# A linear-attention block with a low-rank feed-forward: one root finder chain for two norms, normalizations one at a time, a reordered first double step

## The chip, the cores and the metric

The kernel runs on one NeuronCore of a Trainium2 chip. The core has five engines with an instruction stream each: TensorE (PE, matrix products; PEld are its weight loads), VectorE (DVE), ScalarE (ACT), GpSimd (POOL), and SyncE (SP), which here issues nearly all DMAs. An engine works its stream strictly in order and waits on semaphores for the others. The metric is the time of one execution on the device, in microseconds (us), as the median of several runs.

## The reference

The input x has 4 sequences of 2048 tokens with 512 features, in float32. A layer norm without weights is followed by a linear attention with 16 heads of 32 features, then a second layer norm and a feed-forward of rank 128; both are added to x.

```python
x = L0_attn_x
x = x + attn(_layernorm(x), ...)
x = x + ffn(_layernorm(x), ...)

def attn(x, ln_g, ln_b, W_qkv, b_qkv, W_gate, b_gate, W_proj, b_proj):
    x_norm = (x - mu) * rsqrt(var + EPS) * ln_g + ln_b
    q, k, v = split(x_norm @ W_qkv + b_qkv, 3)
    gate = sigmoid(x @ W_gate + b_gate)
    gate = gate / (mean(gate) + EPS)
    q = relu(q * gate) ** 2 + EPS
    k = relu(k * gate) ** 2 + EPS
    # over the tokens of a sequence, per head:
    #   kv += k v^T;  ks += k;  out = (q kv) / (q ks + EPS)
    return out @ W_proj + b_proj

def ffn(x, U1, V1, b1, U2, V2, b2):
    P = x @ U1                                # 512 -> 128
    H = gelu(P @ V1 + b1)                     # 128 -> 2048
    return (H @ U2) @ V2 + b2                 # 2048 -> 128 -> 512
```

The attention's own norm sits on top of the first layer norm, so each token needs two reciprocal roots for the first norm: one of var + EPS and one of var (1 + EPS) + EPS². The second layer norm needs one.

## The kernel before

**Tiling.** The 8192 tokens are 64 chunks of 128; a sequence is 16 chunks. x stays in a pool of ten tiles of 128 x 512, loaded chunk by chunk. The main loop takes two chunks per turn, c = 4, 6, ..., 62, a *double step*: it computes gates, values, queries and keys of chunks c and c + 1, the attention of chunks e = c - 1 and c, the output projection of chunks e - 1 and e, the second norm of these two, and the feed-forward of a pair further back. Chunks 0 to 3 are done by straight code ahead of the loop.

**Products.** Pairs of chunks are multiplied by a seven-product scheme (`gates_and_values`, `queries_and_keys`, `project_two_out`): sums and differences of features (`combinations`, tile *combos*, four additions on GpSimd, lines 415 to 418) and of weights (`difference`, slots T1 to T4 of *wgv*, *wqk*, *wp*) take the place of an eighth product. In `gates_and_values` the first product is *ps_g* (from the features themselves), the second *ps_gu* (needs *combos*), then a third, and a fourth and fifth that add to the first and third bank after VectorE has read these (*gu*, lines 443 and 447). All of these matmuls appear on line 423, those of `project` on line 379.

**Attention.** Per chunk: `sums_of` scans the keys (VectorE, L591) and multiplies them by the queries (GpSimd, *qsum* L601); `inverse_denominators` turns *qsum* and inverts (*back* L637 to *inv* L652, VectorE); `scores_of` makes four banks *ps_a* which VectorE masks (L625); `weighted` adds the state's part and the scores' part (*ps_n*, *ps_m*, L687 and L698), divides (*oT*, L661) and updates the state (*ps_S* L717, copied L726). `values_of(c)` makes the values of one chunk by four matmuls on PE (each in two passes) and one addition on VectorE (L551); value tiles come from a pool of three.

**Turning.** Queries, keys and normalized chunks have to be transposed. `blocks` turns 32 x 32 blocks on VectorE (L286, a pool of three tiles), and a write to DRAM and reads in another order do the rest: `turned_in_quarters` writes once (L302) and queues four reads (L307), issued by the next `transfers_back`; `turned` writes four times (L325) and queues one read (L330), issued by `features_back`. All of them go through SP's queue, in order.

**Norms.** Means and variances come from VectorE (`moments`). `first_norm_factors` makes the scale, the shift and the factor *unscale* of the first norm for two chunks, from chunk 8 on all on GpSimd: two variances (L349, L350), a start value from the bits of the number (L242), three Newton rounds of four operations (L247 to L250), two operations for *shift_o* (L260, L261), two for *unscale*. `second_norm` does the same for one variance per chunk (L802, L242, L247 to L250, *shift_f*) and returns two functions, one per chunk, which normalize on ScalarE (L267), add the feed-forward's last bias on GpSimd (L812) and turn the result (*x2T*). `normalize_chunk` normalizes a chunk for the first norm (ScalarE, *xl*) and returns a function that turns it.

**Feed-forward.** `feed_forward(b)` returns a list of 21 pieces for a pair of chunks: `down` (*ps_P* L832 from *x2T*, copied to *pT* L843), 18 times `both(f)` (*ps_h* L847, the gelu *h* on ScalarE L849, and two pieces later *ps_Q* L853 from *h*), and `up` twice. `pump(n)` takes the next n pieces; so they are laid between the attention's products.

**What sets the order.** Nothing is scheduled automatically (`manual_schedule`): each engine's stream is in the order in which the Python code calls, and tiles rotate through small pools, where a new tile waits for the last reader of the one it replaces. The part of a double step that the change touches stands, in calls, as follows: `project_two_in_step(e)`, two pieces, `sums_and_products(c)`, `second_norm([e - 1, e])`, `first_norm_factors([c + 4, c + 5])`, two pieces, `scores_in_step(c)`, `denominators_in_step(c)` (which adds a bias to x on GpSimd, L970), four pieces, both normalizations of the second norm, `combine(c + 2)`, the remaining pieces up to `up`, the attention of c, `up`, `sums_and_products(c + 1)`, `normalize_pair(c + 4)`.

Of the kernel before, what the change touches and what calls it, by code (L numbers as in the profile page):

```python
# [52 lines left out]
ALU = mybir.AluOpType  # L53
# [3 lines left out]
EPS = 1e-5  # L57
# [3 lines left out]
def tile_linear_attention_block(  # L61
# [19 lines left out]
    nc = tc.nc  # L81
# [8 lines left out]
    NJ = 4  # L90
    NP = 2
    BT = NP * P
    NC = B * T // P
# [87 lines left out]
    for g in range(NK):  # L181
        halves = w_proj[bass.ts(g, P), :].rearrange("(two p) n -> two p n", two=2)
        for half in range(2):
            at = (half ^ (g % 2)) * (P // 2)
# [44 lines left out]
    def inverse_root(v, tag, name):  # L229
        n = v.shape[-1]  # L230
        sd = work.tile([P, 2 * NJ], F32, tag="sd", bufs=2, name=f"sd_{name}")[:, 0:n]
        nc.scalar.activation(sd, v, AF.Sqrt)
        rs = work.tile([P, 2 * NJ], F32, tag=tag, bufs=5, name=f"{tag}_{name}")[:, 0:n]
        nc.vector.reciprocal(rs, sd)
        return rs
# [17 lines left out]
    def variances(n, name):  # L253
        return work.tile([P, 2 * NJ], F32, tag="newton_v", bufs=2, name=f"v_{name}")[:, 0:n]

    def normalizer(mean, rs, name, engine):

        n = rs.shape[-1]
        shift = work.tile([P, NJ], F32, tag="shift", bufs=6, name=f"shift_{name}")[:, 0:n]
        engine.tensor_mul(shift, mean, rs)  # L260
        engine.tensor_scalar_mul(shift, shift, -1.0)  # L261
        return rs, shift

    def normalized(src, norm, j, name):
        t = temp(name)
        rs, shift = norm
        nc.scalar.activation(  # L267
            t, src, AF.Identity, scale=rs[:, j : j + 1], bias=shift[:, j : j + 1]
        )
        return t  # L270
# [24 lines left out]
    def transfers_back():  # L295
        while back:
            back.pop(0)()
# [18 lines left out]
    def features_back():  # L316
        while features:
            features.pop(0)()
# [19 lines left out]
    def first_norm_factors(chunks, mv):  # L338

        n = len(chunks)
        at = slice(chunks[0] % NJ, chunks[-1] % NJ + 1)
        name = str(chunks[0])
        inverse, engine = inverse_root_by_steps, nc.gpsimd
        if chunks[0] < 2 * NJ:
            inverse, engine = inverse_root, nc.vector
        v = variances(2 * n, name)
        engine.tensor_scalar_add(v[:, 0:n], mv[:, at, 1], EPS)  # L349
        engine.tensor_scalar(v[:, n:], mv[:, at, 1], 1.0 + EPS, EPS * EPS, ALU.mult, ALU.add)  # L350
        rs = inverse(v, "rs_o", name)
        norm = normalizer(mv[:, at, 0], rs[:, n:], f"o{name}", engine)
        back = work.tile([P, NJ], F32, tag="unscale", bufs=2, name=f"unscale_{name}")[:, 0:n]
        engine.tensor_mul(back, rs[:, 0:n], rs[:, n:])
        engine.tensor_mul(back, back, v[:, n:])
        for n, c in enumerate(chunks):
            first_norm[c] = norm, n, back[:, n : n + 1]
# [18 lines left out]
    def project(c, w, name):  # L376
        ps = bank(name)
        for k in range(NK):
            nc.tensor.matmul(
                ps, xlT_of[c][:, k, :], w[k], start=(k == 0), stop=(k == NK - 1)  # L380
            )
        return ps
# [165 lines left out]
    def values_of(c):  # L548
        ps = project(c, rows_of[2], f"ps_v_{c}")
        values[c] = v = new_values(c)  # L550
        nc.vector.tensor_add(v, ps, bqkv_row[:, 2 * D : 3 * D])  # L551

    def new_values(c):
        return work.tile([P, D], F32, tag="v", bufs=3, name=f"v_{c}")
# [239 lines left out]

    x2T_of = {}

    def second_norm(chunks, mv):

        at = slice(chunks[0] % NJ, chunks[-1] % NJ + 1)
        name = str(chunks[0])  # L800
        v = variances(len(chunks), f"f{name}")
        nc.gpsimd.tensor_scalar_add(v, mv[:, at, 1], EPS)  # L802
        rs = inverse_root_by_steps(v, "rs_f", name)
        norm = normalizer(mv[:, at, 0], rs, f"f{name}", nc.gpsimd)

        def normalize(n, c):
            b, j = divmod(c, NP)
            if b not in x2T_of:
                x2T_of[b] = work.tile([P, NP, NQ, NK, DH], F32, tag="x2T", name=f"x2T_{b}")
            xt = x_of[c]  # L810
            x2 = normalized(xt, norm, n, f"x2_{c}")
            nc.gpsimd.tensor_add(xt, xt, b2_row)  # L812
            to = x2T_of[b][:, j]
            if c < NC - 2:
                turned_in_quarters(x2, to, f"x2_{c}")
                return None

            return lambda: nc.scalar.copy(
                to.rearrange("p i k t -> p k i t"),
                features_first(x2, f"ps_x2_{c}").rearrange("p k (i t) -> p k i t", t=DH),  # L820
            )

        return [lambda n=n, c=c: normalize(n, c) for n, c in enumerate(chunks)]
# [60 lines left out]
    def pump(n):  # L884
        for _ in range(min(n, len(rest))):
            rest.pop(0)()
# [47 lines left out]
    mv_first = mv_second = None  # L934
# [3 lines left out]
    combos = {}  # L938
    results = {}
    waiting = []  # L940

    def combine(c):
        combos[c] = combinations(c)
# [11 lines left out]
    def new_keys_in_step(c):  # L955
        kT = new_keys(c)
        keys_of(kT, pairs[c][2])
        keys[c] = kT, None

    def sums_and_products(c):  # L960
        if c not in keys:
            new_keys_in_step(c)
        kT = keys[c][0]
        keys[c] = kT, sums_of(c, kT, pairs[c][1])

    def scores_in_step(e):
        return scores_of(e, pairs[e][1], keys[e][0])

    def denominators_in_step(e):
        nc.gpsimd.tensor_add(x_of[e], x_of[e], bp_row)  # L970
        return inverse_denominators(e, keys[e][1])
# [22 lines left out]
    def normalize_pair(c):  # L994
        if c < NC:
            return [normalize_chunk(n) for n in (c, c + 1)]
        return []
# [26 lines left out]
    mv = new_moments("mv_0")  # L1024
# [9 lines left out]
    turn_xl = normalize_chunk(1)  # L1034
# [4 lines left out]
    turn_xl = [normalize_chunk(c) for c in (2, 3)]  # L1039
# [24 lines left out]
    second = queries_and_keys(0, combos.pop(0), later=moments_meanwhile)  # L1064
# [7 lines left out]
    turn_xl = normalize_pair(NJ)  # L1072
# [11 lines left out]
    def scores_of_first():  # L1084
# [4 lines left out]
    second = queries_and_keys(  # L1089
        2,  # L1090
        combos.pop(2),
        sums_of_first,
        factors,
        scores_of_first,
        lambda: new_keys_in_step(1),
    )
    inv = denominators_in_step(0)
    rest_of_attention(0, held["scores"], inv)
    sums_and_products(1)
    scores = scores_in_step(1)  # L1100
    combine(NJ)
    new_keys_in_step(2)
    inv = denominators_in_step(1)
    values_of(3)
    project_in_step(0)
    for to in (T1, T2, T4, T3):
        difference(wgv, to, nc.gpsimd)
# [2 lines left out]
    scores = scores_in_step(2)  # L1110
# [10 lines left out]
    for c in range(NJ, NC, 2):  # L1121

        e = c - 1
        for n in (c + 4, c + 5):
            if n < NC:
                load_x(n)
        held = {}

        def denominators():
            held["inv"] = denominators_in_step(e)  # L1130

        later = c == NJ
        if later:
            gates_and_values(c, combos[c], lambda: new_keys_in_step(e))
            sums_and_products(e)
            while waiting:
                waiting.pop(0)()
            transfers_back()
            turn_xl = normalize_pair(c + 2)
        else:  # L1140
            gates_and_values(c, combos[c], denominators)
        scores = scores_in_step(e)

        def turn_features():
            for turn in turn_xl:
                turn()

        second = queries_and_keys(c, combos.pop(c), queries=turn_features if later else None)

        rest += feed_forward((c - 4) // NP)  # L1150
        pump(1)
        if later:
            denominators()
        rest_of_attention(e, scores, held["inv"])
        combine_results(e)
        features_back()
        second()
        for n in (c + 4, c + 5):
            first_moments(n)
        pump(4)  # L1160
        project_two_in_step(e)
        transfers_back()
        pump(2)
        sums_and_products(c)
        waiting += second_norm([e - 1, e], mv_second)
        if c + 4 < NC:
            first_norm_factors([c + 4, c + 5], mv_first)
        pump(2)


        scores = scores_in_step(c)
        inv = denominators_in_step(c)
        pump(4)
        while waiting:
            waiting.pop(0)()
        transfers_back()
        if c + 2 < NC:
            combine(c + 2)
        pump(len(rest) - NP)
        rest_of_attention(c, scores, inv)  # L1180
        if c + 2 < NC:
            pump(len(rest))
            sums_and_products(c + 1)
        for turn in normalize_pair(c + 4):
            turn()


    e = NC - 1
    new_keys_in_step(e)
    scores = scores_in_step(e)  # L1190
# [71 lines left out]
```

## Time and profile before

| | us |
|---|---|
| median of 3 runs | 1853.89 |
| lowest and highest of them | 1851.64, 1854.89 |
| the profiled execution | 1857.51 |
| its span, first to last instruction | 1855.7 |
| TensorE busy in it | 1787.7 |
| VectorE busy | 1321.7 |
| GpSimd busy | 907.2 |
| ScalarE busy | 665.9 |
| mean granted TensorE clock, as a share | 0.996 |

All the times inside an execution come from that one profiled execution, counted from its first instruction. A line of a timeline gives the start, the duration, the engine, the source line, the operation, *written <- read* tiles with their shapes and the number of instructions that were merged, and in brackets the idle time of the engine before it with what ended it. A line of the waits gives who waited for whom, the total in us, how many times, and the longest. A line of the stretches gives the stretch, its length, the busy time of PE, PEld, DVE, ACT and POOL with the number of instructions, the granted TensorE clock as a share, the share of the DMA engines' time, and GB/s. Matmuls overlap in the array, so the durations of neighbours add up to more than the distance of their starts; distances of starts are the better measure.

A steady double step, from one *ps_gu* to the next (1008.56 to 1065.31 us), takes 56.75 us, and 28 to 30 of them make up the loop.

### The profile page before, as it was taken

To read this page: it belongs to the slowest core of one execution; us is meant where nothing else is said; L and a number is where in the kernel's file an instruction comes from. 1 tells how busy PE (TensorE), PEld (TensorE's weight loads), DVE (VectorE), ACT (ScalarE), POOL (GpSimd) and SP (SyncE) were. 2 spreads that over 40 slices of the span, in tenths; PEclk is the share of its full clock that TensorE was granted. 3 is DMA by queue.
4 is the path that set the end of the run, shared out by engine and by line. 5 is a ranking of instruction groups with operands and counts; after the bars stand their busy time and mean duration, and the time that the engine had idled before them with its cause. 6 is when DMAs were issued, how large, how long until landed. Compare 5 with 4: busy or idle time off the path is not lost.

```text
span 1855.7 us, 35857 instructions
## 1 busy us (share of the span) xinstructions
PE 1787.7 (96%) x13112; PEld 1128.1 (61%) x13112; DVE 1321.7 (71%) x2579; ACT 665.9 (36%) x1203; POOL 907.2 (49%) x1761
## 2 busy tenths in 40 slices
PE   9899999999999999999999999999999999999998
PEld 4555666655666556665556665566655566655667
DVE  7887767777768677677777686776777776867662
ACT  4333334333433333343334333333423333333333
POOL 3565454454554455544545544555445455445441
PEclk9999999999999999999999999999999999999999
DMA  7132332323322323322233223232222332232220
GB/s 227 62 105 86 101 99 89 91 87 99 108 90 82 99 86 102 98 90 89 87 99 110 89 82 98 86 103 96 88 91 88 96 111 89 83 98 76 80 81 23
DMA packets 286132, 173.81 MB, mean 94 GB/s; under 512 B 134654, under 2 KB 235518, under 8 KB 285828
## 3 DMA queue, kind: packets, MB, share of 16 engines
q1 hardware_dynamic: 284894, 171.51, 29.6%
q8 instruction: 104, 1.70, 0.4%
q14 instruction: 72, 0.59, 0.1%
q10 hardware_dynamic: 1062, 0.01, 0.0%
HBM read 89.68 MB, written 81.79 MB: 92 GB/s over the span
## 4 chain that ended last, share of the span: by engine, by line
PE 61%; POOL 22%; DVE 10%; issue 6%; ACT 1%; DMA 0%; SPq 0%; DVEq 0%; POOLq 0%; ACTq 0%
PE ps_q L423 11%; PE ps_g L423 8%; PE ps_h L847 4%; POOL x L812 4%; PE ps_gu L423 3%; PE ps_p L423 3%; PE ps_t L423 3%; PE ps_k L423 3%; PE ps_pt L423 3%; PE ps_Q L853 3%; PE ps_P L832 3%; PE ps_v L423 3%; PE ps_gt L423 3%; PE ps_u L423 3%; DVE st L226 2%
## 5 line engine op out<-in xcount | busy, mean ns | idle before, releaser
L849 ACT ACTIVATE h<-ps_h,b_col 128x256 f32<-128x256 f32 x512 | 227.6, 468 | 304.7 <-PE ps_h L847 304.4
L853 PE MATMUL ps_Q<-h,u_sb 128*128 128x256 f32 x1024 | 302.5, 387 | 31.8 <-ACT h L849 31.8
L847 PE MATMUL ps_h<-pT,v_sb 128*128 128x256 f32 x1024 | 302.3, 387 | 1.3 <-DVE pT L843 1.3
L853 PEld LDWEIGHTS ps_Q<-h,u_sb 128*128 128x128 f32 x1024 | 187.4, 190 | 82.8 <-ACT h L849 61.0
L601 POOL TENSOR_TENSOR qsum<-qT,sums 128x512 f32<-128x512 f32 x64 | 75.4, 1178 | 314.7 <-DVE sums L591 310.5
L847 PEld LDWEIGHTS ps_h<-pT,v_sb 128*128 128x128 f32 x1024 | 190.8, 191 | 32.6 <-DVE pT L843 2.8
L423 PE MATMUL ps_q<-wqk,xlT 128*128 128x512 f32 x372 | 179.7, 606 | 2.7 <-DVE t L501 2.6
L625 DVE TENSOR_TENSOR a<-ps_a,causal 128x512 f32<-128x512 f32 x256 | 158.3, 680 | 24.1 <-PE ps_a L615 24.1
L423 PE MATMUL ps_g<-wgv,xlT 128*128 128x512 f32 x360 | 170.0, 601 | 0.9 <-DVE gu L447 0.9
L520 POOL TENSOR_TENSOR u<-u,t 128x512 f32<-128x512 f32 x32 | 40.7, 1272 | 204.4 <-DVE t L518 198.0
L591 DVE TENSOR_TENSOR_SCAN sums<-keep,kT 128x516 f32<-128x516 f32 x64 | 80.1, 1251 | 85.0 <-POOL kT L575 85.0
L567 POOL TENSOR_SCALAR k<-k 128x512 f32<-128x512 f32 x64 | 96.2, 1504 | 82.3 <-DVE blocks_k L286 82.3
L402 ACT ACTIVATE gate<-gate 128x512 f32<-128x512 f32 x64 | 40.2, 629 | 236.7 <-DVE gate L398 236.6
L423 PEld LDWEIGHTS ps_g<-wgv,xlT 128*128 128x128 f32 x360 | 65.9, 190 | 94.6 <-issue 71.8
L470 POOL TENSOR_TENSOR v<-gu,g 128x512 f32<-128x512 f32 x30 | 38.1, 1271 | 167.9 <-DVE g L465 167.9
L423 PEld LDWEIGHTS ps_q<-wqk,xlT 128*128 128x128 f32 x372 | 67.2, 191 | 83.5 <-issue 53.3
L491 ACT ACTIVATE t<-t,rg 128x512 f32<-128x512 f32 x32 | 23.1, 722 | 200.0 <-DVE t L489 200.0
L226 DVE BATCH_NORM_STATS2 st<-x 128x6 f32<-128x512 f32 x128 | 86.6, 676 | 8.6 <-DMA x<-in_L_attn_x_dram 6.4
L495 ACT ACTIVATE k<-u,rg 128x512 f32<-128x512 f32 x64 | 45.7, 714 | 119.1 <-DVE u L489 119.1
L615 PEld LDWEIGHTS ps_a<-qT,kT 32*128 32x128 f32 x2048 | 63.3, 186 | 33.4 <-issue 21.2
L970 POOL TENSOR_TENSOR x<-x,bp_row 128x512 f32<-128x512 f32 x64 | 82.2, 1284 | 0.0
L812 POOL TENSOR_TENSOR x<-x,b_row 128x512 f32<-128x512 f32 x64 | 79.9, 1272 | 0.9 <-ACT x L267 0.9
(199 smaller groups left out, 3673.6 us busy)
## 6 DMA issues: line engine op xcount, KB each, us to landing
x<-in_L_attn_x_dram SPq DMA_DIRECT2D x64, 256.0 KB
dr_q<-blocks_q SPq DMA_DIRECT2D x64, 256.0 KB
dr_k<-blocks_k SPq DMA_DIRECT2D x64, 256.0 KB
qT<-dr_q SPq DMA_DIRECT2D x256, 64.0 KB
kq<-dr_k SPq DMA_DIRECT2D x256, 64.0 KB
out_dram<-x SPq DMA_DIRECT2D x64, 256.0 KB
dr_x<-blocks_x SPq DMA_DIRECT2D x62, 256.0 KB
x2T<-dr_x SPq DMA_DIRECT2D x248, 64.0 KB
```

The costliest lines, as they stand in the source:

```text
L226: nc.vector.bn_stats(st, src)
L423: nc.tensor.matmul(ps, stationary[:, k, :], w[:, slot, k, :], start=(k == 0 and not more), stop=(k == NH - 1), skip_group_check=True,)
L567: nc.gpsimd.tensor_scalar_add(k, k, EPS)
L591: nc.vector.tensor_tensor_scan(sums.rearrange(flat), keep.rearrange(flat), kT.rearrange(flat), 0.0, ALU.mult, ALU.add,)
L601: nc.gpsimd.tensor_mul(qs.rearrange("p k (i t) -> p k i t", t=DH), qT.rearrange("p i k t -> p k i t"), sums[:, :, 1 : P + 1].rearrange("p ...
L615: nc.tensor.matmul(ps[r][:, bass.ts(g, P)], kT[rows, g, 1 : P + 1], qT[rows, :, g, :], start=True, stop=True,)
L625: nc.vector.tensor_tensor(a, ps[r].rearrange("p (g t) -> p g t", t=P), causal.unsqueeze(1).to_broadcast([P, NK, P]), ALU.mult,)
L812: nc.gpsimd.tensor_add(xt, xt, b2_row)
L847: nc.tensor.matmul(ps, v1_sb[:, 0, bass.ts(f, P)], held["p"], start=True, stop=True)
L849: nc.scalar.activation(h, ps, AF.Gelu_apprx_tanh, bias=b1_col[:, f : f + 1])
L853: nc.tensor.matmul(held["q"], u2_sb[:, f, :], held["h"].pop(f), start=(f == 0), stop=(f == NF - 1))
L970: nc.gpsimd.tensor_add(x_of[e], x_of[e], bp_row)
```

## The change

Four things are changed.

- *One chain for both norms.* `second_norm` takes the chunks of the first norm as well (`others`) and their moments. It puts all their variances beside its own in one tile (two columns become six), runs one start value and one set of Newton rounds over all, makes *shift_f*, and then calls the new function `both_factors`, the tail that was part of `first_norm_factors`. The call of `first_norm_factors` in the loop is gone. For the last two double steps there are no others.
- *Normalizations one by one.* Where both functions of the second norm were called together between the feed-forward's pieces, one is called, then two pieces follow, then the other.
- *Ahead of the loop*, `values_of(3)` moves from behind `denominators_in_step(1)` to just ahead of `denominators_in_step(0)` and chunk 0's attention.
- *In the first double step* (c = 4), `sums_and_products(3)` moves from ahead of the scores into `queries_and_keys`, behind the first query's product; the waiting normalizations of chunks 0 and 1 and the reads they queue move behind the first addition of `queries_and_keys`; the normalization and the turns of chunks 6 and 7 move from `queries_and_keys` to behind `second()`, followed by their reads.

```diff
     def first_norm_factors(chunks, mv):
...
-        inverse, engine = inverse_root_by_steps, nc.gpsimd
-        if chunks[0] < 2 * NJ:
-            inverse, engine = inverse_root, nc.vector
+        engine = nc.vector
         v = variances(2 * n, name)
         engine.tensor_scalar_add(v[:, 0:n], mv[:, at, 1], EPS)
         engine.tensor_scalar(v[:, n:], mv[:, at, 1], 1.0 + EPS, EPS * EPS, ALU.mult, ALU.add)
-        rs = inverse(v, "rs_o", name)
+        both_factors(chunks, mv, v, inverse_root(v, "rs_o", name), engine)
+
+    def both_factors(chunks, mv, v, rs, engine):
+        n = len(chunks)
+        at = slice(chunks[0] % NJ, chunks[-1] % NJ + 1)
+        name = str(chunks[0])
         norm = normalizer(mv[:, at, 0], rs[:, n:], f"o{name}", engine)
         back = work.tile([P, NJ], F32, tag="unscale", bufs=2, name=f"unscale_{name}")[:, 0:n]
         engine.tensor_mul(back, rs[:, 0:n], rs[:, n:])
...
-    def second_norm(chunks, mv):
+    def second_norm(chunks, mv, others=(), mv_others=None):
...
-        v = variances(len(chunks), f"f{name}")
-        nc.gpsimd.tensor_scalar_add(v, mv[:, at, 1], EPS)
+        n, m = len(chunks), len(others)
+        v = variances(n + 2 * m, f"f{name}")
+        nc.gpsimd.tensor_scalar_add(v[:, 0:n], mv[:, at, 1], EPS)
+        if others:
+            var = mv_others[:, others[0] % NJ : others[-1] % NJ + 1, 1]
+            nc.gpsimd.tensor_scalar_add(v[:, n : n + m], var, EPS)
+            nc.gpsimd.tensor_scalar(
+                v[:, n + m :], var, 1.0 + EPS, EPS * EPS, ALU.mult, ALU.add
+            )
         rs = inverse_root_by_steps(v, "rs_f", name)
-        norm = normalizer(mv[:, at, 0], rs, f"f{name}", nc.gpsimd)
+        norm = normalizer(mv[:, at, 0], rs[:, 0:n], f"f{name}", nc.gpsimd)
+        if others:
+            both_factors(others, mv_others, v[:, n:], rs[:, n:], nc.gpsimd)
...
         lambda: new_keys_in_step(1),
     )
+    values_of(3)
     inv = denominators_in_step(0)
     rest_of_attention(0, held["scores"], inv)
...
     inv = denominators_in_step(1)
-    values_of(3)
     project_in_step(0)
...
         if later:
             gates_and_values(c, combos[c], lambda: new_keys_in_step(e))
-            sums_and_products(e)
-            while waiting:
-                waiting.pop(0)()
-            transfers_back()
-            turn_xl = normalize_pair(c + 2)
+
+            def normalized_first():
+                while waiting:
+                    waiting.pop(0)()
+                transfers_back()
+
+            scores = scores_in_step(e)
+            second = queries_and_keys(
+                c,
+                combos.pop(c),
+                first=normalized_first,
+                queries=lambda: sums_and_products(e),
+            )
         else:
             gates_and_values(c, combos[c], denominators)
-        scores = scores_in_step(e)
...
-        second = queries_and_keys(c, combos.pop(c), queries=turn_features if later else None)
+            scores = scores_in_step(e)
+            second = queries_and_keys(c, combos.pop(c))
...
         second()
+        if later:
+            for turn in normalize_pair(c + 2):
+                turn()
+            features_back()
...
-        waiting += second_norm([e - 1, e], mv_second)
-        if c + 4 < NC:
-            first_norm_factors([c + 4, c + 5], mv_first)
+        others = [c + 4, c + 5] if c + 4 < NC else []
+        waiting += second_norm([e - 1, e], mv_second, others, mv_first)
         pump(2)
...
         pump(4)
-        while waiting:
-            waiting.pop(0)()
+        waiting.pop(0)()
+        pump(2)
+        waiting.pop(0)()
         transfers_back()
```

More of the change, by code (lines that the diff above doesn't have):

```diff
@@ L1134, in tile_linear_attention_block @@
             gates_and_values(c, combos[c], lambda: new_keys_in_step(e))
-            sums_and_products(e)
-            while waiting:
-                waiting.pop(0)()
-            transfers_back()
-            turn_xl = normalize_pair(c + 2)
+            def normalized_first():
[9 more added lines that the diff above has]
+            )
         else:
             gates_and_values(c, combos[c], denominators)
-        scores = scores_in_step(e)
-        def turn_features():
-            for turn in turn_xl:
-                turn()
-        second = queries_and_keys(c, combos.pop(c), queries=turn_features if later else None)
+            scores = scores_in_step(e)
+            second = queries_and_keys(c, combos.pop(c))
         rest += feed_forward((c - 4) // NP)
```

## The prediction

> **What bounds the kernel now.** First the page's busy shares and its chain that ended last; the chain names the engines that set the end.
>
> ```profile
> PE 1787.7 (96%) x13112; PEld 1128.1 (61%) x13112; DVE 1321.7 (71%) x2579; ACT 665.9 (36%) x1203; POOL 907.2 (49%) x1761
> PE 61%; POOL 22%; DVE 10%; issue 6%; ACT 1%; DMA 0%; SPq 0%; DVEq 0%; POOLq 0%; ACTq 0%
> ```
>
> TensorE (PE) is busy for 96%, so without new arithmetic there are at most 1855.7 - 1787.7 = 68 us to win. But 22% of the chain is GpSimd (POOL), which is busy for only 49%: it matters somewhere. The view of waits, PE alone, says where PE stands still; its first two rows hold 47.7 us:
>
> ```profile
> PE ps_Q L853 <- ACT h L849: 31.8, 30, 1.1
> PE ps_gu L423 <- POOL combos L416: 15.9, 28, 1.1
> ```
>
> Both come once per double step. The timelines of PE, POOL and ACT in one ordinary double step (56.75 us long) show them:
>
> ```profile
> 1054.92 0.23 POOL L349 TENSOR_SCALAR v<-mv 128x2 f32<-128x2 f32 x1
> 1055.21 0.19 POOL L350 TENSOR_SCALAR v<-mv 128x2 f32<-128x2 f32 x1
> 1055.48 0.19 POOL L242 TENSOR_SCALAR rs_o<-v 128x4 int32<-128x4 int32 x1
> ...
> 1054.87 1.52 ACT L267 ACTIVATE x<-x,shift_f,rs_f 128x512 f32<-128x512 f32 x2 [1.14 <-POOL shift_f L261]
> 1056.30 1.18 ACT L849 ACTIVATE h<-ps_h,b_col 128x256 f32<-128x256 f32 x3
> ...
> 1056.81 0.70 PE L853 MATMUL ps_Q<-h,u_sb 128*128 128x256 f32 x2 [1.05 <-ACT h L849]
> 1057.34 0.59 PE L847 MATMUL ps_h<-pT,v_sb 128*128 128x256 f32 x2
> ...
> 1006.17 1.88 PE L423 MATMUL ps_g<-wgv,xlT 128*128 128x512 f32 x4
> 1008.56 1.98 PE L423 MATMUL ps_gu<-wgv,combos 128*128 128x512 f32 x4 [0.51 <-POOL combos L416]
> 1010.38 1.88 PE L423 MATMUL ps_g<-wgv,combos 128*128 128x512 f32 x4
> ```
>
> GpSimd's root finder for the second norm ends with shift_f; ScalarE waits for it, normalizes two chunks, and only then makes the h that PE's ps_Q needs. GpSimd meanwhile does a second root finder (rs_o), three additions and the combinations, and PE's ps_gu waits for these. Last, PE in the first double step, whose order also changes, with the stretch view of the granted clock:
>
> ```profile
> 75.38 5.40 PE L379 MATMUL ps_v<-wgv,xlT_early 128*128 128x512 f32 x8 [3.66 <-DVE oT L661]
> 100.62 1.98 PE L423 MATMUL ps_g<-wgv,xlT 128*128 128x512 f32 x4 [0.61 <-DVE gu L447]
> 113.38 3.53 PE L423 MATMUL ps_q<-wqk,xlT 128*128 128x512 f32 x4 [2.60 <-DVE t L501]
> ...
> 75.56:78.97 3.41, 3.41 (x5) 1.35 (x6) 3.41 (x7) 0.00 (x0) 1.84 (x2) 0.50 0.25 75
> 113.11:116.52 3.41, 3.14 (x4) 1.51 (x5) 0.90 (x2) 0.00 (x0) 0.70 (x1) 0.50 0.24 73
> ```
>
> After both long stalls the granted clock (the column before the last two) is 0.50 for 3.41 us: four matmuls take 3.53 us instead of 1.88, so such a stall costs up to 1.7 us more.
>
> **One chain for both norms** (28 double steps, c = 4 to 58). Removed from GpSimd: one start value (L242) and 12 steps. From L349 at 1054.92 to the end of unscale at 1060.03 the old stretch takes 5.1 us, from v_f at 1050.42 on 9.61 us. The new one: three variances 0.86, L242 0.28, 12 steps on 6 columns, four operations for shift_f and shift_o and two for unscale, together 1.48. A step takes 0.2775 us on 2 columns and 0.2817 on 4 (3.33 and 3.38 us for 12), so I take 0.286 on 6, 3.43 us. Sum 6.05, so all behind it comes 3.56 us earlier. L416 ended at about 1008.51; it will end at 1004.95, and PE wants ps_gu at 1006.17 + 1.82 = 1007.99. The wait is gone with 3.0 us to spare. Price: a stall is worth its idle time, 0.06 of modelled end (2.39 us from ps_g to ps_gu, instead of 1.82 and 0.51) and 0.10 of refill (ps_gu to the next 1.82, otherwise 1.72). So 15.9 + 28 x 0.16 = **-20.4 us**. What is hidden now: VectorE's sums wait for kT L575 behind these combinations (3 us each); they come earlier too, and PE's next look at VectorE (gu L447) gets easier.
>
> **The two normalizations, one by one.** shift_f now stands behind two more variances and wider steps: 0.56 + 0.10 + 0.01 = 0.67 us later. ScalarE's first normalization starts at 1055.54 instead of 1054.87; the next h no longer waits for the second (0.715): 1056.255 against 1056.30, and ps_Q starts 0.05 us earlier. The second normalization now stands between the h: it begins at 1056.965, the h behind it at 1057.68, its ps_Q at 1058.19, where PE wants 1058.165: 0.03 lost. Net -0.02 x 28 = **-0.6 us**. Bounds: were the second normalization to hide fully and shift_f late by nothing, -0.7 each, which the POOL rows exclude; I take -0.25 to +0.35 each, -7 to +10. The later second turn (VectorE blocks_x +1.35 us, then its copy on SP and eight x2T reads) lies 20 us ahead of its reader ps_P, and GpSimd reaches the addition that must follow it (L812) at 1058.97, after 1057.7. For c = 60 nothing is fused: 0.7 us gained, **-0.7**; for c = 62 the tail's ps_P waits 2.01 us for the x2T transfer, which does not move: 0.
>
> **First double step.** (a) values_of(3) moves ahead of chunk 0's attention. Its 8 matmuls (3.43 us) fill the idle time before 75.38. But v_3 takes the buffer of v_0 (a pool of three), so VectorE's addition L551 waits until chunk 0's last ps_S matmul: 68.47 (the end of ps_q at 66.75 + 1.72) + 3.43 + 1.4 (ps_n to ps_S) = 73.3, with its own 0.65 us 74.0. Behind it in VectorE's order stand back L637 (71.76 before, now 74.0), inv, oT, sums; behind sums GpSimd's qsum, combinations, the wgv differences (10.39 us) and qsum of chunk 2; behind that gu L447 and PE's ps_g at 100.62. All slip by 2.25: PE waits until 102.87, idle 3.2 us. (b) Putting sums and the turns behind the score products frees t L501: the stall of 2.60 at 113.38 and its half clock go. From 102.87 the unstalled sequence (11.72 us) brings ps_t to 114.6, or 116.3 after a half clock, against 116.74. (c) The same move makes the turns of x2 late: behind t L501, 3.6 to 5.3 us later. The eight x2T reads moved 75 GB/s from 113 to 120 and now land at 123.6 to 125.3, so ps_P, at 123.61 before, starts at 123.8 to 125.5, a half clock (1.7) possible behind it. (d) The turns of chunks 6 and 7, with eight writes and two reads on SP, now follow second(): 1.43 us on ScalarE ahead of h (at most 0.4 seen by PE), and blocks_xl of chunk 7 uses the buffer of blocks_q of chunk 5, whose write queues behind the kq reads: 1 to 2 us on VectorE, which then holds PE's output products. Sum of (c) and (d) at the ends: 0.2 + 0 and 1.9 + 1.7 + 2.4; the low end is below nothing if the late turns hide, -2. I take **+2.6**, range -2 to +6.
>
> The Trainium skill (page "TensorE: Matmul & The Clock Gate", section "HAM oscillation — how this bites in real kernels") says that only idle gaps above about 3.4 us throttle PE again. Here a stall of 2.60 us did, so the trace decides. By that rule the stalls of (a) and (c) would cost no half clock, and the sum would be about 1 us lower.
>
> **Sum:** -20.4 - 0.6 - 0.7 + 2.6 = -19.1 us against the profiled execution: span 1855.7 to 1836.6, its 1857.5 us to 1838.4. That execution lay 3.6 us above the median of the runs; on their scale 1853.9 - 19.1 = **1834.8**.
>
> **Rivals.** *The h wait goes as well.* If the root chain's extra 0.67 us is hidden, ps_Q gains 0.7 per step: 1834.8 - 20 = 1815. For it: 31.8 us stand in that row. Against it: the 1.14 us that ScalarE idles for shift_f is time measured from shift_f, and that is later. 7%.
> *The gain is given back at the second normalization.* If ScalarE has no slack there, each step loses up to 0.715 - 0.13 = 0.58: +16, 1851. For it: ScalarE feeds PE one h per 0.86 us in this place. Against: three h follow each other at 0.355. 5%.
> *Half clock in every step (slower).* A stretch of 3.41 us with 1.51 us idle (58.50 to 61.91) kept the full clock, one with 2.33 lost it. If the wait at ps_Q grows from 1.07 past about 1.75, that is by 0.67 and no h moved ahead, each step pays 1.7 more: 28 x (1.7 + 0.67) = 66, so 1835 + 66 = 1901. It decides from 0.7 us more idle; I find 0.05 less. 5%.
> *It doesn't do what it says.* If combos L415 waits for something other than its own engine, say the xlT transfer, the 20.4 stay: 1855. Against: its row of waits names only ACT, once. 3%.
>
> **How the numbers follow.** Forecast 80%, 1834.8; its own bounds are 1834.8 - 4.6 - 6.4 and + 3.4 + 10.6 if the two uncertain terms both end at one side, which is unlikely, so 1827 to 1843 in most cases. The range, 1825 to 1843, takes in these and the way towards the first rival; the other rivals (13%) and the far corners stay out. 0.2%, 3.7 us, is what a measurement can tell from no change: faster holds the forecast, the first rival and a little of the second, 88%; same the rest of the second and part of the fourth, 6%; slower 6%.
>
> **What would show it.** Right: no PE row for combos L416; POOL some 364 instructions fewer; PE's idle time at ps_Q near 1.0 per step; a double step of 56.1 us; PE waiting near 102 for gu L447 and near 123 for x2T. Wrong: a new row of PE with 28 entries, 0.50 of the clock inside the loop, or a double step still at 56.75.

## The result and the profile after

The changed kernel takes 1828.99 us (median of 4 runs, 1826.79 to 1830.76) where the kernel before takes 1854.37 on the same chip: a ratio of 0.9866, 95% interval 0.9848 to 0.9883. The 25.4 us are more than the 19.1 that were forecast, and the time lies 5.8 us under the forecast 1834.8. A second set of runs of the changed kernel gave 1828.23 and 0.9861 (0.9845 to 0.9878).

The page of the changed kernel (busy shares, the chain that ended last), and its view of waits, PE alone:

```profile
span 1825.0 us, 35492 instructions
PE 1776.5 (97%) x13112; PEld 1133.1 (62%) x13112; DVE 1320.5 (72%) x2579; ACT 659.8 (36%) x1203; POOL 834.6 (46%) x1397
PE 91%; DVE 4%; ACT 1%; issue 1%; DMA 1%; POOL 1%; SPq 0%; ACTq 0%; DVEq 0%; POOLq 0%
```

```profile
PE ps_Q L865 <- ACT h L861: 25.4, 30, 1.1
PE ps_g L426 <- DVE gu L450: 3.6, 1, 3.6
PE ps_P L844 <- DMA dr_q<-blocks_q: 2.5, 1, 2.5
PE ps_P L844 <- DMA out_dram<-x: 2.4, 1, 2.4
PE ps_p L740 <- DVE oT L664: 2.3, 1, 2.3
```

GpSimd issues 364 instructions fewer (1761 to 1397) and has left the chain that sets the end (22% to 1%). The row *ps_gu <- combos* with its 28 entries is gone; the row *ps_Q <- h* is still there, a fifth smaller. Of the four rows below it, *gu*, *dr_q* and *oT* belong to the first double step and the stretch ahead of it, *out_dram* to the tail. The wait put down to *dr_q* is that of *ps_P* for *x2T*: SP issues the eight reads of *x2T* from 116.68 us on, and *dr_q* right behind them, at 121.30; in the profile with values_of(3) late, below, the same wait is put down to *x2T*. So of the signs named ahead, the missing row, the 364 instructions and the waits near 102 and 123 came; the idle time at *ps_Q* came out at 0.87 instead of 1.0 per step and the double step at 55.72 instead of 56.1, as the next lines show.

One ordinary double step of the changed kernel, from its timelines of PE, ACT and POOL:

```profile
1050.04 1.88 PE L426 MATMUL ps_gu<-wgv,combos 128*128 128x512 f32 x4
1096.35 0.59 PE L859 MATMUL ps_h<-pT,v_sb 128*128 128x256 f32 x2
1097.81 0.70 PE L865 MATMUL ps_Q<-h,u_sb 128*128 128x256 f32 x2 [0.87 <-ACT h L861]
1098.78 1.59 PE L865 MATMUL ps_Q<-h,u_sb 128*128 128x256 f32 x6
1100.30 0.31 PE L690 MATMUL ps_n<-qT,S 32*32 32x128 f32 x4
1105.76 1.88 PE L426 MATMUL ps_gu<-wgv,combos 128*128 128x512 f32 x4
...
1096.59 0.81 ACT L267 ACTIVATE x<-x,shift_f,rs_f 128x512 f32<-128x512 f32 x1 [1.66 <-DVE inv L655]
1097.31 0.82 ACT L861 ACTIVATE h<-ps_h,b_col 128x256 f32<-128x256 f32 x2
1098.02 0.81 ACT L267 ACTIVATE x<-x,shift_f,rs_f 128x512 f32<-128x512 f32 x1
...
1096.33 0.23 POOL L261 TENSOR_SCALAR shift_f<-shift_f 128x2 f32<-128x2 f32 x1
1101.91 0.73 POOL L419 TENSOR_TENSOR combos<-combos,xlT 128x256 f32<-128x256 f32 x1
```

The double step takes 1105.76 - 1050.04 = 55.72 us, 1.03 less than before. The combination that *ps_gu* reads ends at 1101.91 + 0.73 = 1102.64, 3.1 us ahead of its reader. ScalarE starts the first normalization at 1096.59, as *shift_f* ends at 1096.56 (the view names VectorE's *inv*, which happened to end at 1096.58; with five Newton steps, below, the same row names *shift_f*, long after *inv*). The h then come between the two normalizations, as the order has it.

### The profile page after: what moved, and what is told of

Read it like the earlier page. It is cut to its first block, busy times and chain, and to the rows that moved or that the text cites. A ratio compares the mean times of both kernels' runs of the same rounds, so it can differ in the third digit from the quotient of the medians.

```text
span 1825.0 us, 35492 instructions
## 1 busy us (share of the span) xinstructions
PE 1776.5 (97%) x13112; PEld 1133.1 (62%) x13112; DVE 1320.5 (72%) x2579; ACT 659.8 (36%) x1203; POOL 834.6 (46%) x1397
## 4 chain that ended last, share of the span: by engine, by line
PE 91%; DVE 4%; ACT 1%; issue 1%; DMA 1%; POOL 1%; SPq 0%; ACTq 0%; DVEq 0%; POOLq 0%
PE ps_Q L865 13%; PE ps_h L859 12%; PE ps_q L426 11%; PE ps_g L426 11%; PE ps_a L618 4%; PE ps_u L883 3%; PE ps_pt L426 3%; PE ps_p L426 3%; PE ps_t L426 3%; PE ps_k L426 3%; PE ps_v L426 3%; PE ps_u L426 3%; PE ps_gt L426 3%; PE ps_pv L426 3%; PE ps_P L844 3%; PE ps_gu L426 3%
## 5 line engine op out<-in xcount | busy, mean ns | idle before, releaser
L865 PE MATMUL ps_Q<-h,u_sb 128*128 128x256 f32 x1024 | 304.7, 388 | 25.4 <-ACT h L861 25.4
L426 PE MATMUL ps_g<-wgv,xlT 128*128 128x512 f32 x360 | 166.2, 597 | 3.6 <-DVE gu L450 3.6
```

Of the source, the lines that this page charges most:

```text
L426: nc.tensor.matmul(ps, stationary[:, k, :], w[:, slot, k, :], start=(k == 0 and not more), stop=(k == NH - 1), skip_group_check=True,)
L865: nc.tensor.matmul(held["q"], u2_sb[:, f, :], held["h"].pop(f), start=(f == 0), stop=(f == NF - 1))
```

## The experiments

Each kernel was run beside the kernel before on the same chip. First, what each part is worth in a double step. Distances of starts on PE, in us, in one ordinary step (c = 36, in the changed kernel c = 38):

| stretch of the double step | before | one chain alone | one by one alone | changed | both later |
|---|---|---|---|---|---|
| ps_gu to ps_gt | 7.16 | 6.87 | 7.16 | 6.86 | 6.86 |
| ps_gt to ps_pt | 23.46 | 23.46 | 23.47 | 23.47 | 23.46 |
| ps_pt to ps_u (holds ps_Q) | 21.93 | 22.42 | 21.30 | 21.85 | 20.61 |
| ps_u to the next ps_gu | 4.20 | 3.54 | 4.76 | 3.54 | 3.54 |
| whole step | 56.75 | 56.29 | 56.69 | 55.72 | 54.47 |

**One chain alone.** The changed kernel with these two places put back:

```diff
-        waiting.pop(0)()
-        pump(2)
-        waiting.pop(0)()
+        while waiting:
+            waiting.pop(0)()
         transfers_back()
```

and the first double step in its old order (the diff of the third experiment).

> The changed kernel with the one chain for both norms alone: the two normalizations stand together again and the first double step has its old order. My theory: PE's row for combos is gone and with it 0.95 us per double step (0.66 from ps_u to ps_gu, 0.29 from ps_gu to ps_gt), but shift_f comes 0.54 us later and nothing is moved ahead of the h, so the idle time at ps_Q grows from 1.05 to 1.6: a double step of 56.75 - 0.95 + 0.54 = 56.35, some 11 us faster than before in all, ratio 0.994. Rival (half clock): 1.6 us of idle time halves the clock in each step, 28 x (1.7 - 0.4): 36 us slower, ratio 1.02. Rival (ScalarE's h have room): the 0.54 is hidden, 26 us faster, ratio 0.986, and the second part of the change does nothing.

Measured: 1840.22 against 1855.54 us, ratio 0.9919 (0.9904 to 0.9934). The timeline of PE:

```profile
1045.98 0.70 PE L865 MATMUL ps_Q<-h,u_sb 128*128 128x256 f32 x2 [1.54 <-ACT h L861]
1052.10 1.88 PE L426 MATMUL ps_g<-wgv,xlT 128*128 128x512 f32 x4
1053.82 1.88 PE L426 MATMUL ps_gu<-wgv,combos 128*128 128x512 f32 x4
```

The wait of *ps_gu* is gone and the one at *ps_Q* has grown from 1.05 to 1.54: the wider chain delivers *shift_f* some 0.5 us later, and nothing hides that. The step gains 0.46. No step of the loop ran at half clock in this profile, so stalls of 1.54 us did not halve it here.

**One by one alone.** The kernel before with the opposite edit.

> The kernel before with the normalizations one by one alone (two chains, old first double step). My theory: the idle time at ps_Q falls from 1.06 to some 0.4, but GpSimd's way from qsum to the combinations does not start earlier for it, so ps_gu starts when it did and its wait grows from 0.51 to some 1.2: the double step stays at 56.75, only the last two steps gain 0.7 each; ratio 0.999. Rival (the parts add up): each gains by itself, 0.6 us per step, 17 us faster, ratio 0.991, step 56.15.

Measured: 1853.75 against 1855.54 us, ratio 0.9993 (0.9981 to 1.0005). Its timeline of PE:

```profile
1055.32 0.70 PE L853 MATMUL ps_Q<-h,u_sb 128*128 128x256 f32 x2 [0.33 <-ACT h L849]
1061.54 1.88 PE L423 MATMUL ps_g<-wgv,xlT 128*128 128x512 f32 x4
1064.48 1.98 PE L423 MATMUL ps_gu<-wgv,combos 128*128 128x512 f32 x4 [1.06 <-POOL combos L416]
```

The wait at *ps_Q* fell by 0.72 us and the one at *ps_gu* rose by 0.55: GpSimd's way from *qsum* to the combinations does not depend on *ps_Q*, so a PE that gets there earlier waits longer. Alone the parts bring 0.46 and 0.06 us per step; together 1.03. The one-by-one order is worth 0.57 (56.29 to 55.72) once the combinations no longer hold PE, and 0.06 while they do.

**The first double step in its old order,** everything else as changed (the whole of these hunks undone; the second is shortened):

```diff
-    values_of(3)
     inv = denominators_in_step(0)
...
     inv = denominators_in_step(1)
+    values_of(3)
...
-            scores = scores_in_step(e)
-            second = queries_and_keys(c, combos.pop(c), first=normalized_first,
-                                      queries=lambda: sums_and_products(e))
+            sums_and_products(e)
+            while waiting:
+                waiting.pop(0)()
+            transfers_back()
+            turn_xl = normalize_pair(c + 2)
```

> The changed kernel with the first double step in its old order, everything else as changed. My theory: the new order costs 3.9 us, so this is 3.9 us faster than the changed kernel (1825 where that has 1829; ratio to before 0.984), with the waits of 3.7 at 75, 0.6 at 100 and 2.6 at 113 back, no wait at ps_P, and double steps of 55.71 as in the changed kernel. Rival (the new order pays): it is slower than the changed kernel by 2 us or more.

**values_of(3) alone put back** (the first half of that diff).

> The changed kernel with values_of(3) alone put back behind the second chunk's denominators. My theory: VectorE's addition of v_3 no longer holds back, inv, oT and sums, so PE's wait for gu near 102 falls from 3.6 to under 1 and its half clock goes, but ps_P still waits for the x2T reads, which come only some 2 us earlier: 1 to 3 us faster than the changed kernel (1826 to 1828), most of the 3.6 us reappearing at ps_P. Rival (values_of(3) is the whole cost): 4 us faster, like the old order. Rival (its 3.4 us of PE work in an idle place is worth more than the delay): slower than the changed kernel by 1 to 3 us.

Measured, on the same chip against 1855.54 us: the old order 1823.59, ratio 0.9836 (0.9819 to 0.9853); values_of(3) alone put back 1824.74, ratio 0.9835 (0.9819 to 0.9851). Both lie 3.5 to 5.4 us below the changed kernel's medians of 1828.99 and 1828.23, though the intervals overlap a little with its own. My theory for the second of them, that most of its gain would come back at *ps_P*, fell: by the medians, moving values_of(3) was the whole cost. The same edit on top of the later normalizations, below, brings 5.5 us with intervals that part. The changed kernel shows how the cost comes about, in the timelines of VectorE and PE:

```profile
73.26 0.69 DVE L554 TENSOR_TENSOR v<-ps_v,bqkv_row 128x512 f32<-128x512 f32 x1 [1.61 <-PE ps_S L720]
73.87 0.70 DVE L640 STREAM_TRANSPOSE back<-qsum 128x512 f32<-128x512 f32 x1
...
102.81 3.50 PE L426 MATMUL ps_g<-wgv,xlT 128*128 128x512 f32 x4 [3.59 <-DVE gu L450]
125.60 3.00 PE L844 MATMUL ps_P<-x2T,u_sb 128*128 128x256 f32 x8 [2.54 <-DMA dr_q<-blocks_q]
```

The addition of v_3 waits for the last product that reads v_0, and *back* behind it starts at 73.87, where it started at 71.76 before. 29 us later PE waits 3.59 for gu, and four matmuls that take 1.88 us otherwise take 3.50. With values_of(3) late, the profile has:

```profile
101.05 1.98 PE L426 MATMUL ps_g<-wgv,xlT 128*128 128x512 f32 x4 [0.56 <-DVE gu L450]
122.82 2.43 PE L844 MATMUL ps_P<-x2T,u_sb 128*128 128x256 f32 x8 [3.03 <-DMA x2T<-dr_x]
```

The wait for gu is back at 0.56 at full clock, and *ps_P* starts 2.8 us earlier than in the changed kernel, although this execution was 0.6 us behind it at 67 us.

**Both normalizations two feed-forward steps later.** What remained at *ps_Q* is a chain that ends at *shift_f* while ScalarE stands idle in front of it.

```diff
-        pump(4)
+        pump(6)
         waiting.pop(0)()
         pump(2)
         waiting.pop(0)()
```

> The changed kernel with both normalizations two feed-forward steps later (pump(6) for pump(4) ahead of the first one). My theory: what is left at ps_Q is shift_f, ready only at 1096.56 while ScalarE stood 1.66 us idle waiting for it with two more h that it could have made; with these ahead of it, gathers and h run without a stall, ps_n comes 1.25 us earlier, and the combinations, whose second one was done 3.1 us ahead of ps_gu, still come in time: a double step of 54.5, some 35 us faster than the changed kernel (1794; ratio to before 0.967). Rival (the gain turns into the combinations' wait, as before the change): the addition that must follow the later normalization and the combinations behind it come later, PE's row for combos returns with some 0.5 us or more: 15 us faster (1814). Rival (the transfer of x2 comes too late for ps_P): a new row of ps_P with 28 entries, no gain.

Measured: 1797.45 against 1852.80 us, ratio 0.9698 (0.9683 to 0.9712). Its timelines of PE, ACT and POOL:

```profile
1022.29 0.59 PE L859 MATMUL ps_h<-pT,v_sb 128*128 128x256 f32 x2
1022.72 1.49 PE L865 MATMUL ps_Q<-h,u_sb 128*128 128x256 f32 x6
1029.59 1.88 PE L426 MATMUL ps_gu<-wgv,combos 128*128 128x512 f32 x4
...
1021.63 0.81 ACT L267 ACTIVATE x<-x,shift_f,rs_f 128x512 f32<-128x512 f32 x1
1022.35 0.45 ACT L861 ACTIVATE h<-ps_h,b_col 128x256 f32<-128x256 f32 x1
...
1021.37 0.23 POOL L261 TENSOR_SCALAR shift_f<-shift_f 128x2 f32<-128x2 f32 x1
1026.95 0.73 POOL L419 TENSOR_TENSOR combos<-combos,xlT 128x256 f32<-128x256 f32 x1
```

The two h more that ScalarE makes first fill its idle time (no bracket at 1021.63), *shift_f* is done at 1021.60, just in time, and PE has no stall at all between the starts of two double steps: 54.47 us, 1.25 less. The combinations end at 1027.68, still 1.9 us ahead of *ps_gu*. Neither rival occurred.

**Later normalizations and values_of(3) late together.**

> The changed kernel with both normalizations two feed-forward steps later and values_of(3) put back behind the second chunk's denominators. My theory: the two add, being at different places: 4 us faster than with the later normalizations alone (1790, ratio to before 0.965). Rival (one stall takes the place of the other): no faster than with the later normalizations alone.

Measured, against the same 1852.80 us: 1791.92, ratio 0.9665 (0.9651 to 0.9680), 5.5 us below the kernel with the later normalizations alone: they add, and the intervals just part. In the tail, *ps_P* waits 3.9 us here and 4.2 with the later normalizations alone, instead of 2.4 and 2.9 in two profiles of the changed kernel. So two more:

```diff
-        pump(6)
+        pump(6 if c + 2 < NC else 4)
```

> As with both normalizations later and values_of(3) late, but in the last double step (c = 62) the normalizations stay where the changed kernel has them, two feed-forward steps earlier. My theory: in the tail ps_P waits for the transfer of these two chunks' x2 (3.9 us with the later place, 2.4 to 2.9 with the earlier), so their place costs there what it gains: ps_Q's 0.35 us comes back, the wait at ps_P falls by some 1.5, and with it one of the three windows at half clock (up to 1.7): 1 to 3 us faster, 1789 to 1791, ratio to before 0.965 to 0.966. Rival (a wait falls away only to be waited for elsewhere in the tail): the same time.

> The same with the first double step wholly in its old order. My theory: once values_of(3) stands late, the other orders of the first double step are worth nothing on their own (ps_q's wait of 2.6 to 2.9 us goes and ps_P's of 2.7 to 3.0 comes): the same as the kernel beside it within 2 us. Rival (the new orders pay): 2 to 4 us slower than it.

Measured, against 1854.58 us: 1790.57, ratio 0.9658 (0.9645 to 0.9671), and with the old first double step 1788.90, ratio 0.9650 (0.9637 to 0.9664). The wait in the tail fell to 2.3 us, and the half clock behind it from three windows to one in the profiled execution, but 1.3 us of the median are within what the runs spread. The two first double steps cannot be told apart: the reordering of the change, other than values_of(3), is worth nothing measurable. Either version is some 3.5% faster than the kernel before and some 2% faster than the changed one (0.9650 / 0.9866 = 0.978, 0.9658 / 0.9866 = 0.979).

**Five Newton steps.** To see what longer stalls do to the clock:

```diff
-        for _ in range(3):
+        for _ in range(5):
```

> The changed kernel with five Newton steps instead of three (eight more operations on GpSimd in each root chain, 2.26 us). My theory: the chain ends at shift_f, so the idle time at ps_Q grows by 2.26 to 3.1 in each double step, and where more than some 2.1 of it fall into one window of 3.413 us of the throttle, the next window runs at half clock; by chance that is 6 steps in 10, so 30 x 2.3 + 17 x 1.5 = 94 us slower than the changed kernel: 1923, granted clock 0.97. Rival (no half clock in the loop): 69 us slower, 1898. Rival (the half clock in every step): 1943. Rival (the chain is not what ps_Q waits for): the same as the changed kernel.

Measured: 1913.27 us (2 runs, 1908.09 and 1918.46), ratio 1.0323 (1.0284 to 1.0361). The step is 57.97 us, 2.25 more than in the changed kernel, all of it at *ps_Q* (3.12 us idle), and ScalarE's row reads 3.93 us idle before the first normalization, ended by *shift_f*: that the root chain sets that wait is shown. But of 31 stalls at *ps_Q* in the profiled execution only 6 were followed by a half clock, where I expected 17. The stretch view around two stalls of the same length, cut at the windows:

```profile
498.74:502.15 3.41, 1.60 (x8) 1.07 (x6) 1.19 (x4) 0.00 (x0) 2.42 (x13) 1.00 0.27 81
502.15:505.56 3.41, 2.08 (x9) 1.64 (x10) 1.42 (x2) 3.30 (x7) 3.25 (x8) 1.00 0.21 78
556.77:560.18 3.41, 0.97 (x5) 0.51 (x3) 0.61 (x1) 0.55 (x1) 2.51 (x13) 1.00 0.25 76
560.18:563.60 3.42, 2.74 (x7) 2.21 (x8) 1.42 (x2) 2.62 (x7) 3.34 (x5) 0.50 0.25 93
```

The stall of 500.34 to 503.48 lies 1.81 us in one window and 1.33 in the next: the clock stays. The one of 557.74 to 560.86 lies 2.44 in one window: the next runs at 0.50. My count of 17 took the positions for random; a step of 57.97 us is 16.98 windows, so the position hardly moves from step to step, and most stalls were split about in halves. That is how the grid fell in this one execution (1908.09 us, granted clock 0.990). The other one took 10 us longer at a granted clock of 0.982, which is some 20 windows of 3.413 us at half clock against 11 over the whole execution; it has no trace, so how many of its stalls were halved stays open.

**The changed kernel once more.**

> The changed kernel itself once more, on the same chip as these. My theory: the time differs from run to run by up to 7 us because a stall of some 2 to 2.6 us in the first double step or the tail halves the clock or does not, as it falls across the throttle's windows: the double steps stay at 55.71 in this profile too, and the windows at half clock are others than the three of the first profile. Rival (what differs is the double steps): they are not 55.71 here.

Measured: 1828.23 us (1826.82 to 1831.36); the profiled execution has a span of 1829.6 where the first one had 1825.0. Its double steps are 55.68. The first profile ran at half clock from 78.6, 102.5 and 126.4, one window each; this one from 86.8, 103.9, 127.8 and, in the tail, from 1776.4 for three windows: six windows against three, 10.2 us more at half clock, where up to half of the time is lost. The 4.6 us lie in the tail alone: the last *ps_gu* starts at 1718.07 here and at 1718.14 in the first profile, and from there to the end it takes 111.5 us against 106.9. Of these, 0.5 is a longer wait of *ps_P* (2.94 instead of 2.41); the rest fits the three windows at half clock.

## Why the prediction was right, and where its size was off

Counted in the two profiled executions up to the last *ps_gu* (c = 62), the change gains 27.5 us (1745.65 to 1718.14), where 19.1 were forecast.

| term | forecast | measured in the profiles |
|---|---|---|
| the wait for the combinations, 28 times | -20.4 | -20.4 at ps_u to ps_gu, -8.5 from ps_gu to ps_gt |
| normalizations one by one, with c = 60 | -0.6 - 0.7 | -2.5 |
| first double step and what is ahead of it | +2.6 | +3.9 |
| sum up to c = 62 | -19.1 | -27.5 |

(Each is the sum over the steps of what a stretch of the table of distances lost. -20.4: 25 steps at 0.66 to 0.67, three at 1.26, where the wait was longer. -8.5: 0.29 in each of 28 steps and 0.35 more in one, c = 16. -2.5: the stretch from ps_pt to ps_u is 0.08 shorter in most steps, 1.9 over 27 of them, and 0.6 shorter at c = 60. +3.9: the first step is 4.07 longer, of which 0.65 is one of the 28 gains, and it starts 0.80 earlier: 4.07 + 0.65 - 0.80.)

**The combinations' wait:** the mechanism was right, and the term was mis-sized by 8.5 us: 28.9 instead of 20.4. Two things were left out. The first is VectorE. The prediction says that VectorE's sums wait behind the combinations "3 us each" and that "PE's next look at VectorE (gu L447) gets easier", but gives it no price. The kernel before, VectorE and PE:

```profile
1010.04 1.23 DVE L591 TENSOR_TENSOR_SCAN sums<-keep,kT 128x516 f32<-128x516 f32 x1 [2.98 <-POOL kT L575]
1013.15 0.69 DVE L447 TENSOR_TENSOR gu<-ps_g,gu 128x512 f32<-128x512 f32 x1
1012.10 3.79 PE L423 MATMUL ps_g<-wgv,xlT 128*128 128x512 f32 x8
1015.72 1.88 PE L423 MATMUL ps_gt<-wgv,combos 128*128 128x512 f32 x4
```

Eight matmuls from 1012.10 should be done 2 x 1.72 = 3.44 us later, and take 3.62: the last four add to the bank that *gu* reads until 1013.84, just later than PE could start them at 1013.82. In the trace's single matmuls the fifth starts at 1013.90, 0.09 late, and the sixth follows it by 0.53 instead of 0.43. This is a stall of 0.19 us inside one merged row, under no bracket and in no row of the waits. The changed kernel:

```profile
1053.67 0.69 DVE L450 TENSOR_TENSOR gu<-ps_g,gu 128x512 f32<-128x512 f32 x1 [0.96 <-PE ps_g L426]
1053.47 3.60 PE L426 MATMUL ps_g<-wgv,xlT 128*128 128x512 f32 x8
1056.90 1.88 PE L426 MATMUL ps_gt<-wgv,combos 128*128 128x512 f32 x4
```

Here *gu* ends at 1054.36, 0.8 us before the fifth matmul starts, and the distance is 1056.90 - 1053.47 = 3.43. The 0.19 us times 28 are 5.3 us, the largest part of what the forecast missed. The experiment with one chain alone has it too (6.87 instead of 7.16), so it belongs to the chain. The second is that I took 1.82 us for the undisturbed distance from ps_g to ps_gu, which itself holds a refill; it is 1.72 (1050.04 - 1048.32 in the changed kernel), 0.1 more per step, 2.8 us in all. The rest, 0.35, is the one step c = 16, of which I don't know the cause.

**The normalizations:** *shift_f* came 0.53 us later (4.95 us from the start of *v_f* to its end, where it was 4.42), not 0.67: a step on six columns takes the 0.282 us of one on four, not 0.286, and two more variances cost 0.45 instead of 0.56. So *ps_Q* gained 0.18 instead of 0.05, and the h behind the second normalization lost 0.11 instead of 0.03. The small net is the difference of two large ones, as the first two experiments show: 0.49 lost by the chain and 0.57 won back by the order. Neither the rival that takes the gain back nor the half clock in each step took place. The rival "the h wait goes as well" needed two feed-forward steps more, which then brought the 1.25 us per step.

**The first double step:** the steps (a) to (d) went as described: the addition of v_3 ends at 73.95 (74.0 forecast), PE waits until 102.81 (102.87), no wait at *ps_q*, *ps_P* at 125.60 (123.8 to 125.5) with a half clock behind it, and the turn of chunk 7 waits 0.97 us for the write of chunk 5's queries. The +2.6 was a middle value; the wait at *ps_P* and the half clock behind it came near the upper ends of (c), 2.0 and some 1.4 us, and (d) cost PE some 0.6 of the 2.4 allowed for, so that +3.9 was measured.

**The base, and some luck.** By the medians the gain is 25.4 us, in the profiles it is 1855.7 - 1825.0 = 30.7: the profiled execution of the kernel before lies 3.1 us above its median of four, and that of the changed kernel 2.2 below. The prediction treated the former as a plain shift. Of the 30.7 us, 27.5 lie up to the last *ps_gu*, and 3.2 behind it, where the kernel before ran two windows at half clock and the changed one none, behind waits of the same kind (2.01 and 2.41 us). In the profiles, from which the terms were worked out, the forecast of 19.1 us misses by 8.4 up to the last *ps_gu*; that the median came within 5.8 us of 1834.8 is in part luck.

## What to carry to other kernels

What two edits bring together can be more than the sum of what each brings alone (1.03 us against 0.46 and 0.06 here): where PE waits in two places of one loop, coming earlier to the second only lengthens the wait there, until that one is gone too. So try the parts together, and look for what a third engine stands idle for. Where an engine waits for a late result, first put the work that needs nothing from it ahead of the wait; here one number, pump(6) for pump(4), brought more than the whole change. In a merged row, compare the distance of starts with the count times the undisturbed one: stalls of 0.2 us are in no bracket and no row of the waits, and 28 of them were a fifth of the gain. And an instruction moved earlier in a strictly ordered stream takes its buffer's wait along, which everything behind it then pays.

## What the hardware showed that was not expected

In all twelve profiles the throttle works on a fixed grid of 3.413 us: all half clocks of one execution begin at whole multiples of it from each other (78.6, 102.5, 126.4 in the changed kernel: seven windows apart each), and behind a window that is idle enough the next one runs at half clock. In the kernel with five Newton steps the six stalls of *ps_Q* that lie with at least 2.07 us in one window were followed by a half clock (of one window four times, of two twice), and the other 25, with at most 1.92 us in one window, by none. In this execution the idle time within one window thus tells them apart: the stall of 3.1 us that is split 1.81 and 1.33 is followed by no half clock. The Trainium skill (page "TensorE: Matmul & The Clock Gate", section "HAM oscillation — how this bites in real kernels") gives gaps of more than some 3.4 us as what throttles; the runs here show the half clock already after stalls of 2.0 to 2.6 us, and none after many gaps of 3.1 that two windows share. The edge is not sharp in idle time alone: in the second profile of the changed kernel the half clock also came behind a window with 1.74 us of PE work, 71 small matmuls, and 1.67 us idle.

```profile
83.36:86.77 3.41, 1.74 (x71) 1.47 (x60) 3.21 (x9) 0.00 (x0) 3.41 (x4) 1.00 0.00 0
86.77:90.18 3.41, 3.41 (x17) 2.65 (x10) 3.41 (x8) 0.00 (x0) 3.33 (x2) 0.50 0.00 0
```

That most products in it use 32 rows or columns of the array may be why; no run here tells it apart. Over the twelve profiles, from 45 us after the start to 8 us before the end, every window at full clock with 2.0 us idle or more was followed by a half clock, and between 1.55 and 2.0 both occurred: 1.55 us (58.73 to 62.14 with the old first double step) halved the next window, and 1.98 (1775.02 to 1778.43 in the changed kernel) did not. The grid does not start with the kernel (78.6 is 23.0 windows from its first instruction, 86.8 is 25.4), so a stall of about the same length can be followed by a half clock in one execution and not in the next; in the two profiles of the changed kernel, the wait of *ps_P* in the tail (2.41 and 2.94 us) was followed by none and by three windows, which is most of the 4.6 us between them.
